# A quarter of the probability-value products moved from VectorE to GpSimd, tiles 2 to 7 of a decoder layer

## The chip, the cores and the metric

The kernel runs on one core of a Trainium2 chip. A core has TensorE (PE, matrix products), VectorE (DVE, elementwise work and reductions), ScalarE (ACT, activations and copies), GpSimd (POOL, elementwise work and the issuing of some transfers) and SyncE (SP, here only a queue that issues transfers). Each engine works through its own queue in order; semaphores make one wait for another. On-chip data lie in SBUF, 128 partitions wide, and results of TensorE in PSUM, in eight banks. The metric is the time of one execution on the device in microseconds, and the number quoted is the median of several runs.

## The reference

One decoder layer on x of 2 x 512 tokens with 1024 features, all in fp32: three sublayers, each added to its input and normalised.

- Attention inside each token. Every token has q of 32 dimensions by 32 heads and k, v of 32 dimensions by 8 heads, each head repeated four times. The scores of a token are a 32 x 32 matrix over pairs of dimensions, summed over the heads.
- A product with a context of 1024 x 1024 per batch, both sides quantised to 256 levels.
- A feed-forward layer: relu squared of an up product (2048 wide) into a down product, plus a latent path scaled by the sum of the two largest routing logits, and a layer norm with gamma and beta.

```
q = einsum('bse,edh->bsdh', x, Wq) + bq          # k, v alike, then repeated 4 times over heads
scores = einsum('bsdh,bseh->bsde', q, k) / sqrt(D)
attn = softmax(scores, axis=-1)
out = einsum('bsde,bseh->bsdh', attn, v)         # the product that the change touches
x = layernorm(x + out)
x = layernorm(x + fake_quant(x) @ fake_quant(ctx))
x = layernorm(x + ffn(x))
```

## The kernel before

The 1024 tokens are eight tiles of 128, one token per partition. Since the repeated heads are equal, q is summed over each group of four, so that scores and outputs need only 8 groups (G = 8, D = 32).

*Token path, tile by tile* (`token_path`). `scores` makes four products of q and k, each [128, 2048] (eight dimensions d, 32 dimensions e, eight groups g; L452, tiles named `pqk`), and reduces each over g (L458) into `s`, a [128, 32, 32] tile. `exponentials` takes row maxima (L467), subtracts them (L468) and lets ScalarE exponentiate `s` in place (L471). `attend` sums the exponentials into `den` (L477), takes reciprocals (L479), and makes four products of probabilities and values, again [128, 2048] each (L485, tiles named `pav`): chunk c has the eight dimensions d from 8c, for all g and e. Each is reduced over e (L491) into `o`. L496 divides by `den`; L506 adds `o` to the tile `xc` and sums its rows. All this is VectorE's, apart from the exponentials. The `pqk` and `pav` tiles share two buffers (tag `prod`).

From tile 2 on the normalisation is mostly ScalarE's (`normalise_aside`): `parts` (L324), squares (L329), `ve` (L331), then a power to -1/2 of one element per partition on GpSimd (`rstd`, L333), `shift` (L337) and one pass over the tile (L338). `cross` quantises the tile on ScalarE (L353, L356, L359, L622), lets TensorE turn the codes (`pta`, L630), copies them (L631), multiplies with the context (`py`, L643), and VectorE adds the result to `xc` (L636, L637, L648). A second normalisation follows, and `transpose_f32` lets TensorE turn the tile for the feed-forward layer (L134).

*Feed-forward blocks.* Two tiles make a block. Blocks 0 and 1 go through `ffn`: sixteen "up" products of eight matmuls each (`pu`, L805) into two PSUM banks (`ps_mm`), emptied by ScalarE (relu L821, square L822), four latent products (L834, and L835 on VectorE), then the down products (`pd`, L1035), whose results VectorE normalises (L302, L984, L991). Blocks 2 and 3 go together through `ffn_pair` (L920) and `down_pair` (L1296) in a scheme with fewer multiplications.

*What sets the order.* The program is written as generators. Tiles 0 and 1 run beside the projections and other preparatory products; then the loop at the end of the kernel emits the feed-forward products of blocks 0 and 1 and advances the token path of tiles 2 to 7 by estimated weights, so that both stand interleaved. The Tile framework then schedules each engine's queue by its own estimates of durations; `tc.issue_after` pins some instructions behind others. TensorE's products are pinned to the order in which they are written. GpSimd's queue also issues transfers: `qk` and `v` of the tile two ahead (L175, L176), context tiles (L536), `ln_beta` onto a finished tile (L715) and outputs (L1019).

The pool `more` is opened between the front part and the feed-forward blocks, that is before tile 2's products, and closed after tile 7. Before the change it holds one tile, a third buffer for down weights (tag `wc`).

Of the kernel before, what the change touches and what calls it, by code (L numbers as in the profile page):

```python
# [9 lines left out]
F32 = mybir.dt.float32  # L10
# [6 lines left out]
P = 128  # L17
# [10 lines left out]
def kernel(  # L28
# [24 lines left out]
    nc = tc.nc  # L53

    B, S, E = x.shape
    _, D, H = wq.shape
    G = wk.shape[2]
# [15 lines left out]
    DC = 8  # L73
# [25 lines left out]
    tokp = tokens_only.enter_context(tc.tile_pool(name="tok", bufs=1, side="right"))  # L99
# [127 lines left out]
    for k in range(KE):  # L227

        pool, tag = (work, "work") if k % 3 == 0 else (xpool, "xc")
# [81 lines left out]
    def normalise(t, name):  # L311

        mean, rstd = mean_rstd([t[:, ts(h, HALF)] for h in range(E // HALF)], name)
        return nc.vector.tensor_scalar(t, t, mean, rstd, ALU.subtract, ALU.mult)

    def normalise_aside(t, sums, name):

        n = sums.shape[-1]
        parts = small.tile([P, 2], F32, tag="parts", name=f"parts_{name}")
        minus = parts[:, 0:1]  # L320
        if n > 1:
            minus = small.tile([P, 1], F32, tag="minus", name=f"minus_{name}")
        with behind_acted(True):
            nc.scalar.activation(  # L324
                parts[:, 0:n], sums, AF.Copy, scale=-1.0 / E, accum_out=minus if n > 1 else None
            )
        square = attp.tile([P, E], BF16, tag="square", name=f"square_{name}")
        total = small.tile([P, 1], F32, tag="square", name=f"squares_{name}")
        nc.scalar.activation(square, t, AF.Square, bias=minus, accum_out=total)  # L329
        ve = small.tile([P, 1], F32, tag="ve", name=f"ve_{name}")  # L330
        nc.scalar.activation(ve, total, AF.Identity, scale=1.0 / E, bias=eps)  # L331
        rstd = small.tile([P, 1], F32, tag="rstd", name=f"rstd_{name}")
        nc.gpsimd.tensor_tensor(rstd, ve, neg_half, ALU.pow)  # L333
        yield 3.0
        shift = small.tile([P, 1], F32, tag="shift", name=f"shift_{name}")
        with behind_acted(True):
            nc.scalar.activation(shift, rstd, AF.Identity, scale=minus)  # L337
        return nc.scalar.activation(t, t, AF.Identity, scale=rstd, bias=shift)  # L338
# [136 lines left out]
    def attend(t, xc, s, v):  # L475
        den = small.tile([P, D], F32, tag="den", name=f"den_{t}")
        nc.vector.tensor_reduce(den, s, AX.X, ALU.add)  # L477
        rden = small.tile([P, D], F32, tag="rden", name=f"rden_{t}")
        nc.vector.reciprocal(rden, den)  # L479
        yield 2.0  # L480

        o = tokp.tile([P, D, G], F32, tag="o", name=f"o_{t}")
        for c in range(D // DC):
            prod = tokp.tile([P, DC * D * G], F32, tag="prod", name=f"pav_{t}_{c}", bufs=2)
            nc.vector.tensor_tensor(  # L485
                prod.rearrange("p (d g e) -> p d g e", d=DC, g=G),
                s[:, ts(c, DC), :].unsqueeze(2).to_broadcast([P, DC, G, D]),
                v.unsqueeze(1).to_broadcast([P, DC, G, D]),
                ALU.mult,
            )  # L490
            nc.vector.tensor_reduce(  # L491
                o[:, ts(c, DC), :].rearrange("p d g -> p (d g)"),
                prod.rearrange("p (c e) -> p c e", e=D), AX.X, ALU.add,
            )
            yield 4.6
        nc.vector.tensor_tensor(o, o, rden.unsqueeze(2).to_broadcast([P, D, G]), ALU.mult)  # L496

        x3 = xc.rearrange("p (c j) -> p c j", j=J)
        o3 = o.rearrange("p d g -> p (d g)").unsqueeze(2).to_broadcast([P, DG, J])
        if t == TB - 1:  # L500

            nc.vector.tensor_tensor(x3, x3, o3, ALU.add)
            normalise(xc, f"1_{t}")
        else:
            sums = small.tile([P, 1], F32, tag="sum1", name=f"sum1_{t}")
            nc.vector.scalar_tensor_tensor(x3, x3, 1.0, o3, ALU.mult, ALU.add, accum_out=sums)  # L506
            yield 1.0
            yield from normalise_aside(xc, sums, f"1_{t}")
        yield 3.0
# [151 lines left out]
    def token_path():  # L661
# [25 lines left out]
        for blk in range(NBLK):  # L687
            xcs = []
            x2T = []
            for i in range(TB):  # L690
# [4 lines left out]
                if t == 0:  # L695

                    begin(1)
                    yield next(at[1][2])
                yield from attend(t, xc, done[t], v)
                if t % (S // P) == 0:  # L700
                    b = t // (S // P)
# [677 lines left out]
    pools = {}  # L1379
# [13 lines left out]
    while not ready:  # L1393
        w_tok += advance()
        while rest is not None and w_fill < w_tok:
            more = next(rest, None)
# [69 lines left out]
```

## Time and profile before

| | |
|---|---|
| median of 3 runs | 709.88 us (708.75 to 710.86) |
| span of the profiled execution | 709.9 us |
| `pav` products, L485 | 32 of 2283 ns, 72.5 us |
| their reductions, L491 | 32 of 2266 ns, 72.0 us |
| `pqk` products, L452 | 32 of 2286 ns, 72.5 us |
| small powers on GpSimd, L333 | 21 of 1049 ns on average, 22.0 us |
| "up" products, L805 (`pu`) | 512 records, 113.4 us |
| granted TensorE clock, mean over the span | 0.989 |

The profile is of one execution. Its page gives busy time per engine, then the span in 40 equal slices (each digit is the busy share in tenths), the transfers, the chain of work that ended last and the costliest groups of instructions. A group's row reads: line, engine, operation, output <- inputs, shape, count, busy time and mean duration, and the idle time of the engine in front of it with what ended it. A row of waits reads: who waited on which line for whom, then total us, times, longest. A timeline row reads: start, duration, engine, line, operation, and in brackets the idle time ahead of it and what ended that. A merged row (x2) spans two instructions.

TensorE records each fp32 matmul of the program as two. An engine's busy time on records that overlap is counted once, so that the start-to-start spacing of like instructions is shorter than their duration: two [128, 2048] products on VectorE take 4.49 us, one 2.28.

### The profile page before, as it was taken

What the parts mean: (1) busy time and instruction counts of PE and PEld (TensorE: products, weight loads), DVE (VectorE), ACT (ScalarE), POOL (GpSimd) and SP (SyncE); (2) the same over time, 40 slices, a digit from 0 to 9 for tenths busy, and PEclk for the clock granted to TensorE, in tenths of its full rate; (3) what the DMA queues carried; (4) which work ended last, traced back from release to release, by engine and by line L of the source; (5) the groups of instructions that cost most, each with busy time, mean ns of one, the idle gap of its engine ahead of it and who ended that gap; (6) DMA issues with size and microseconds to landing.
All of it is one profiled execution on the core that took longest, in us unless ns stands there. A gap on an engine that the chain in (4) does not pass through costs nothing. (4 is left out here: it accounts for less than half of the span.)

```text
span 709.9 us, 7428 instructions
## 1 busy us (share of the span) xinstructions
PE 682.9 (96%) x2794; PEld 482.8 (68%) x2794; DVE 587.8 (83%) x678; ACT 262.5 (37%) x440; POOL 78.0 (11%) x107
## 2 busy tenths in 40 slices
PE   6999999999999999999999999989999999999991
PEld 3666654578876444478876444568888888888881
DVE  5799977699999999799999940587677689897785
ACT  2197644322636459426726041122251200000342
POOL 1011212100011122001001000120010000000012
PEclk9999999999999999999999999999999999999996
DMA  9989719395446558346437435697696444557643
GB/s 333 301 253 367 216 23 295 99 301 161 143 133 171 178 195 257 136 158 228 124 118 195 161 119 165 212 275 261 236 338 229 173 153 150 175 180 198 216 90 119
DMA packets 70901, 139.08 MB, mean 196 GB/s; under 512 B 5265, under 2 KB 39697, under 8 KB 70865
## 3 DMA queue, kind: packets, MB, share of 16 engines
q1 hardware_dynamic: 60656, 106.87, 44.7%
q0 software_dynamic: 10064, 31.47, 16.3%
q8 instruction: 22, 0.36, 0.2%
q10 hardware_dynamic: 144, 0.26, 0.1%
q14 instruction: 15, 0.11, 0.1%
HBM read 114.99 MB, written 21.50 MB: 192 GB/s over the span
## 5 line engine op out<-in xcount | busy, mean ns | idle before, releaser
L1035 PE MATMUL pd<-dn,h 128*128 128x512 f32 x320 | 138.9, 592 | 0.0
L805 PE MATMUL pu<-x2T,up 128*128 128x256 f32 x512 | 113.4, 380 | 0.8 <-ACT relu L821 0.8
L1035 PEld LDWEIGHTS pd<-dn,h 128*128 128x128 f32 x320 | 60.3, 190 | 72.7 <-issue 72.2
L805 PEld LDWEIGHTS pu<-x2T,up 128*128 128x128 f32 x512 | 96.4, 190 | 15.2 <-ACT relu L821 1.2
L452 DVE TENSOR_TENSOR pqk<-qk 128x2048 f32<-128x2048 f32 x32 | 72.5, 2286 | 0.0
L485 DVE TENSOR_TENSOR pav<-s,v 128x2048 f32<-128x2048 f32 x32 | 72.5, 2283 | 0.0
L458 DVE TENSOR_REDUCE s<-pqk 128x256 f32<-128x2048 f32 x32 | 72.4, 2281 | 0.1
L491 DVE TENSOR_REDUCE o<-pav 128x64 f32<-128x2048 f32 x32 | 72.0, 2266 | 0.0
L153 PE MATMUL pqk<-wqkv,xT 128*128 128x512 f32 x128 | 66.1, 619 | 1.8 <-DVE wqkv L233 1.5
L158 PEld LDWEIGHTS pv<-wqkv,xT 128*128 128x128 f32 x128 | 24.3, 190 | 24.2 <-issue 22.5
L333 POOL TENSOR_TENSOR rstd<-ve,neg_half 128x1 f32<-128x1 f32 x21 | 22.0, 1049 | 145.2 <-ACT ve L331 141.9
L158 PE MATMUL pv<-wqkv,xT 128*128 128x256 f32 x128 | 35.6, 379 | 0.0
L153 PEld LDWEIGHTS pqk<-wqkv,xT 128*128 128x128 f32 x128 | 24.7, 198 | 13.9 <-issue 8.0
L821 ACT ACTIVATE relu<-pu 128x256 f32<-128x256 f32 x32 | 12.1, 377 | 52.0 <-PE pu L805 52.0
L643 PE MATMUL py<-cq,aT 128*128 128x512 bf16 x128 | 28.9, 379 | 0.9 <-ACT aT L631 0.9
L1200 DVE TENSOR_TENSOR tt<-dn 128x1024 f32<-128x1024 f32 (+1 forms) x20 | 21.2, 1062 | 9.7 <-DMA dn<-tw 4.4
L436 PE MATMUL pe<-fc,exT 128*128 128x512 f32 x64 | 28.7, 594 | 0.0
L805 PE MATMUL pl<-x2T,fc 128*128 128x256 f32 x128 | 28.2, 380 | 0.3 <-ACT latent L834 0.3
L805 PEld LDWEIGHTS pl<-x2T,fc 128*128 128x128 f32 x128 | 24.2, 190 | 4.0 <-ACT latent L834 0.7
L631 ACT COPY aT<-pta 128x1024 bf16<-128x1024 bf16 x7 | 7.0, 1006 | 50.7 <-PE pta L630 50.7
L643 PEld LDWEIGHTS <-aT 128*128 128x128 bf16 x128 | 12.3, 98 | 16.7 <-ACT aT L631 1.7
L302 DVE BATCH_NORM_STATS2 stats_f<-pd 128x6 f32<-128x512 f32 x8 | 5.3, 686 | 20.4 <-PE pd L1035 20.4
(309 smaller groups left out, 1169.8 us busy)
## 6 DMA issues: line engine op xcount, KB each, us to landing
up<-in_L_ffn_up_w_dram SPq DMA_DIRECT2D x16, 1024.0 KB, 5.8
dn<-in_L_ffn_down_w_dram SPq DMA_DIRECT2D x16, 1024.0 KB, 4.9
pair<-in_L_ffn_up_w_dram SPq DMA_DIRECT2D x8, 1024.0 KB, 5.5
dn<-tw SPq DMA_DIRECT2D x8, 1024.0 KB, 5.1
tw<-outer POOLq DMA_DIRECT2D x7, 1024.0 KB, 4.5
fc<-in_L_ffn_fc_w_dram SPq DMA_DIRECT2D x6, 1024.0 KB, 5.7
dn<-in_L_ffn_down_w_dram SPq DMA_DIRECT2D x12, 512.0 KB, 5.3
outer<-in_L_ffn_down_w_dram SPq DMA_DIRECT2D x5, 1024.0 KB, 5.0
```

Source lines behind the costliest of these rows:

```text
L153: projecting[0] = nc.tensor.matmul(pqk, xT[:, k, :], wqkv[k][:, 0 : 2 * DG], start=(k == 0), stop=(k == KE - 1))
L158: nc.tensor.matmul(pv[:, :DG], xT[:, k, :], wqkv[k][:, 2 * DG : 3 * DG], start=(k == 0), stop=(k == KE - 1),)
L333: nc.gpsimd.tensor_tensor(rstd, ve, neg_half, ALU.pow)
L436: expert[0] = nc.tensor.matmul(ps, exT[m // 2][:, m % 2, ts(l, P)], fc2[m // 2][:, m % 2, ts(n, HALF)], start=(m == 0), stop=(m == NL - 1),)
L452: nc.vector.tensor_tensor(prod.rearrange("p (d e g) -> p d e g", d=DC, g=G), q3[:, ts(c, DC), :].unsqueeze(2).to_broadcast([P, DC, D, G]), ...
L458: nc.vector.tensor_reduce(s[:, ts(c, DC), :].rearrange("p d e -> p (d e)"), prod.rearrange("p (c g) -> p c g", g=G), AX.X, ALU.add,)
L485: nc.vector.tensor_tensor(prod.rearrange("p (d g e) -> p d g e", d=DC, g=G), s[:, ts(c, DC), :].unsqueeze(2).to_broadcast([P, DC, G, D]), ...
L491: nc.vector.tensor_reduce(o[:, ts(c, DC), :].rearrange("p d g -> p (d g)"), prod.rearrange("p (c e) -> p c e", e=D), AX.X, ALU.add,)
L643: crossed[t] = nc.tensor.matmul(py, aT[:, k, :], cq[:, k, ts(h, HALF)], start=(k == 0), stop=(k == KC - 1))
L805: lately[0] = nc.tensor.matmul(ps[:, :NB], ws[:, k, wcols], xT[:, k, :], start=(k == 0), stop=(k == KE - 1))
L1035: lately[0] = nc.tensor.matmul(pd[i][n], h[:, kk // 4, i, kk % 4, :], w[:, k, ts(n, HALF)], start=(kk == 0), stop=(kk == NK - 1),)
L1200: nc.vector.tensor_tensor(tt[:, 0:2], w[:, :, 0::3, :].rearrange("p j q n -> p q j n"), b12.unsqueeze(1).to_broadcast([P, 2, nj, QW]), ALU ...
```

## The change

In `attend`, for every tile for which the pool `more` is open (tiles 2 to 7), the fourth chunk's product is issued on GpSimd, ahead of the other three in the program, into a buffer of its own in `more` (tag `aside`, one buffer of 8 KB per partition). The other three products stay on VectorE with their two shared buffers, and all four reductions stay on VectorE. For tiles 0 and 1 nothing changes. What is computed is the same.

```
         o = tokp.tile([P, D, G], F32, tag="o", name=f"o_{t}")
-        for c in range(D // DC):
-            prod = tokp.tile([P, DC * D * G], F32, tag="prod", name=f"pav_{t}_{c}", bufs=2)
-            nc.vector.tensor_tensor(
+        aside = D // DC - 1 if "more" in pools else None
+        prods = {}
+
+        def product(c):
+            beside = c == aside
+            pool, tag, bufs = (pools["more"], "aside", 1) if beside else (tokp, "prod", 2)
+            prods[c] = prod = pool.tile(
+                [P, DC * D * G], F32, tag=tag, name=f"pav_{t}_{c}", bufs=bufs
+            )
+            (nc.gpsimd if beside else nc.vector).tensor_tensor(
                 prod.rearrange("p (d g e) -> p d g e", d=DC, g=G),
                 s[:, ts(c, DC), :].unsqueeze(2).to_broadcast([P, DC, G, D]),
                 v.unsqueeze(1).to_broadcast([P, DC, G, D]),
                 ALU.mult,
             )
+
+        if aside is not None:
+            product(aside)
+        for c in range(D // DC):
+            if c != aside:
+                product(c)
+            prod = prods.pop(c)
             nc.vector.tensor_reduce(
```

In the changed file the products stand on line 492, their reductions on line 505, and everything behind that is 14 lines lower.

## The prediction

> **What bounds the kernel now.** I read the engine totals and their forty slices first, then what TensorE waits for between 120 and 430 us, then the timelines of VectorE, GpSimd and ScalarE around tile 2.
>
> ```profile
> span 709.9 us, 7428 instructions
> ...
> PE 682.9 (96%) x2794; PEld 482.8 (68%) x2794; DVE 587.8 (83%) x678; ACT 262.5 (37%) x440; POOL 78.0 (11%) x107
> ...
> PE   6999999999999999999999999989999999999991
> ...
> DVE  5799977699999999799999940587677689897785
> ```
>
> TensorE is busy from end to end; VectorE is full only from about 135 to 414 us, where it does the attention of tiles 2 to 7 beside the feed-forward products. In that stretch TensorE waits only 2.3 us:
>
> ```profile
> PE py L643 <- ACT aT L631: 0.9, 1, 0.9
> PE pu L805 <- ACT relu L821: 0.8, 1, 0.8
> PE pl L805 <- ACT latent L834: 0.3, 1, 0.3
> PE pta L608 <- DVE a L344: 0.3, 1, 0.3
> ```
>
> All four come from ScalarE or VectorE, so making VectorE shorter can win about 2 us at most; making it later can cost more, if lateness reaches TensorE through ScalarE, which empties TensorE's two banks of the "up" products (`pu`). GpSimd has only small arithmetic, and the timelines show what it does beside VectorE:
>
> ```profile
> 209.55 2.45 POOL L333 TENSOR_TENSOR rstd<-ve,neg_half 128x1 f32<-128x1 f32 x1 [14.79 <-ACT ve L331]
> ```
> ```profile
> 207.08 4.49 DVE L485 TENSOR_TENSOR pav<-s,v 128x2048 f32<-128x2048 f32 x2
> 211.49 0.42 DVE L835 TENSOR_TENSOR h<-latent,rwb 128x256 f32<-128x256 f32 x1
> ```
>
> The same one-element power takes 0.56 us at 302.23, beside statistics read from PSUM. Here it began in the second of two VectorE products (207.08 to 211.57) and ended at 212.00, 0.43 us after it; those at 230.29, 261.43 and 277.87 end 0.42 to 0.43 us after a product too. So a GpSimd operation is held up by a running VectorE product of two SBUF operands. That the reverse holds, this trace can't show: its GpSimd operations are too short.
>
> **The change.** In the built program tiles 2 to 7 each have one product on GpSimd: six leave VectorE (L485 x32 becomes x26). TensorE's and SP's orders are unchanged. The eight-element-row reduction of each GpSimd product stays on VectorE, and stands last or last but one. The buffer is a new one; nothing else gives up room, and no DMA is added: 0 us.
>
> *Removed.* A product costs 2.20 us start to start (four of them with four reductions fill 17.6 us): 6 x 2.20 = 13.2 us of VectorE.
>
> *The GpSimd product, X us.* No row has it. Floor: VectorE's own 2.28 us. The nearest row by engine is the affine select over 128x128, 0.317 us; less 0.098 us for a 128x1 memset it is 0.219 us per 128 elements, so 2048 take 3.5 us, and with the 0.55 us of a small two-operand operation 4.0 us. Ceiling: the second operand is read on its own, 7.0 + 0.55 = 7.5 us. I take 4.0, from the only row that reads and writes a tile.
>
> *The hold-up.* GpSimd's product and VectorE's `den` both wait for the exponentials:
>
> ```profile
> 157.38 1.22 DVE L477 TENSOR_REDUCE den<-s 128x32 f32<-128x1024 f32 x1 [1.12 <-ACT s L471]
> 158.52 2.28 DVE L485 TENSOR_TENSOR pav<-s,v 128x2048 f32<-128x2048 f32 x1
> ```
>
> GpSimd therefore starts during `den`, 1.14 us before VectorE's first product. If the hold-up works both ways, that product waits X - 1.14; the tile nets X - 1.14 - 2.20 = X - 3.34, +0.66 us at 4.0. Bounds: -2.20 (no hold-up) and +4.16 (X = 7.5). I take both ways: the rows show one engine kept out by the other's operands, and none shows VectorE passing a GpSimd operation under way.
>
> On this the Trainium skill, "SBUF — State Buffer", section "Who interferes with whom", says that a VectorE instruction with two SBUF inputs and a GpSimd one that reads SBUF exclude each other for the whole instruction, whichever began first holding. "GPSIMD Engine Reference", section 3.1, gives 4497 ns for a two-operand operation on 2048 fp32 elements; with that X the sum below would be about 727 us, and both pages speak against this change.
>
> *The new queues.* What matters more than 0.66 us is what now stands ahead of what. ScalarE's queue is reordered in the changed program (it assumes an early end of each tile), and GpSimd's has a product ahead of a small power. An "up" product takes TensorE 3.45 us and needs the bank two products back.
>
> ```profile
> 180.91 0.38 ACT L821 ACTIVATE relu<-pu 128x256 f32<-128x256 f32 x1 [2.62 <-PE pu L805]
> 181.33 0.42 ACT L822 ACTIVATE h<-relu 128x256 f32<-128x256 f32 x1
> 182.91 0.20 ACT L324 ACTIVATE parts<-sum 128x1 f32<-128x1 f32 x1 [1.16 <-DVE xc L506]
> 183.14 1.15 ACT L329 ACTIVATE square<-xc,parts 128x1024 bf16<-128x1024 f32 x1
> ```
>
> 1. Tile 2. `parts` and `square` now stand ahead of that relu (fifth pair, second half). `parts` moves to 183.57, the relu ends at 185.43 instead of 181.29; TensorE wants its bank at 180.91 + 3.45 = 184.36: 1.1 us idle. The next relu now stands behind `shift` (rstd), L338 and L353. GpSimd's power, ready at 185.75, falls into VectorE's second `pqk` product (185.65 to 187.94) and ends near 188.37; two passes of 1.27 and `shift` put the relu's end at 191.5; TensorE is ready at 185.4 + 3.45 = 188.9: 2.6 idle (0.6 without that wait). One more relu behind L356, L359 and L622: 0.5. The wait of 0.86 at 201.03 goes, since TensorE is later. Net +3.4.
> 2. Tiles 3 and 4. Before, `xc_3` was normalised by 266.41 and TensorE transposed it at 266.49: no slack. Now ScalarE's `parts` of tile 4 (waits for L506) stands ahead of tile 3's `shift`. Tile 4's `den` starts 2 x 0.66 late, at 246.0; its products wait until 250.0; three products, four reductions, L479, two L648, L496, a `pqk` product and L506 end at 270.9. From L356 to the end of L338 took 3.5 us before (262.91 to 266.41): done at 274.6. TensorE comes at 266.49 + 3.4 = 269.9: +4.7, in all 8.1.
> 3. Second block's start. ScalarE, held there to 270.9, ends its exponentials of tile 5 at 295.8 instead of 290.37 (its 26.4 us from 262.91 to 289.33 less 1.25 for L622, now behind, and 1.6 idle). L648 of tile 4 has the wait of 2.86, a reduction and a `pqk` product (2.20 each) ahead of it and one product less: 5.4 + 5.1 = 10.5 late, to 327.9. Behind it stands ScalarE's chain to two relus: ends at 330.1 and 336.0 (to 337.8 if a power meets a product). TensorE wants them at 321.1 + 8.1 = 329.2 and 333.55: 0.9 + 2.5 to 4.2, less the old 0.78. I take +3.5, in all 11.6.
> 4. Tile 6. Tile 5's power now stands on GpSimd behind tile 6's product, and tile 5's `shift` ahead of a relu on ScalarE. The exponentials stand behind a relu of 339.94 + 11.6, so end at 353.6; product 4.0, then the power behind VectorE's first product 2.6, then 4.4 of ScalarE: 364.6. TensorE is ready at 339.94 + 3 x 3.45 + 11.6 = 361.9: +2.7, in all 14.3.
>
> Tile 7 costs nothing: its codes are ready at 429 and turned at 453.37, 24 us of cover, gone only if VectorE alone fell that far back. GpSimd's DMA issues that stand behind a product (`v`, `qk` for two tiles later) move by at most 4 us and have some 20 us of cover; without it they would delay `pqk`. From 466 us on all is TensorE's as before. The profiled execution's span is 709.9 us, nothing lies around it, and the median of the runs is 709.88. Sum: 709.9 + 3.4 + 4.7 + 3.5 + 2.7 = 724.2, **724 us**. Each us of X moves it by about 5: step 1 by one, 2 by two (three `den` or products less TensorE's own lateness), 3 and 4 by one each.
>
> **Rivals.**
> - *VectorE isn't held up; GpSimd alone gives way.* For it: only that direction is in the rows. VectorE gains 2.20 per tile, but TensorE gets only its waits back (0.86 + 0.78 + 0.28 = 1.9), and step 4 remains: without lateness the power behind a 4.0 us product ends the relu at 351.0 against 350.3, 0.7. 708.7 us.
> - *Faster: the same with a quick product, X = 2.3.* Step 4 goes too: 708.0, and some of the 2.25 us wait of the last transposes would have to go as well to be below 707.8. It decides only if X is below 3.3 and VectorE runs undisturbed; TensorE's 96% speaks against more.
> - *Held up, but X = 2.3.* 724.2 - 1.7 x 5 = 715.7.
> - *Held up and X = 7.5.* 724.2 + 3.5 x 5 = 741.7.
> - *The change doesn't do what it says:* excluded, the six products stand in GpSimd's queue.
>
> **How the numbers follow.** Held up both ways 0.79, of which X from 2.3 to 3.3: 0.12, 3.3 to 5.6: 0.60, above: 0.07. One-sided with X near 4 or more 0.15; with a quick X 0.06. Range: leaving out those above 735 us (X over 6.1, 0.06) and below 709 (about 0.12) gives 709 to 735; the likeliest case's own range is 716 to 732. About 0.3% (2.1 us) can be told from no change. Slower: 0.79 and a little of the one-sided case, 0.80; same 0.14; faster 0.06.
>
> **What would show it.** Right: L492 products on VectorE with a first one per tile of about X + 1.1 us or a gap of 2.9 after `den`; GpSimd rows of 128x2048 near 4 us; TensorE waits for ScalarE's relu near 184, 189, 330 to 340 and 365 us and for `xc` near 270. Step 1 fails if the relu comes before 184.4; step 2 if L506 of tile 4 ends before 266; step 4 if the power is not behind the product. Wrong altogether: first products of 2.28 us right behind `den`, with TensorE's waits unchanged.

## The result, and the profile after

The changed kernel takes 727.23 us (median of 4 runs, 725.11 to 728.20) against 709.62 (four runs) for the kernel before on the same chip: 1.0238 times as long, 95% interval 1.0222 to 1.0254. Forecast were 724.0 us and "slower" with a chance of 0.80. The profiled execution has a span of 725.3 us and a time of 727.1.

The lines of the page that answer to those shown before (span, busy time per engine, slices, and three groups: VectorE's products of probabilities and values, GpSimd's, and the reductions; in a group the columns are shape and count, busy time and mean duration, idle time ahead):

```profile
span 725.3 us, 7422 instructions
...
PE 685.1 (94%) x2794; PEld 484.8 (67%) x2794; DVE 595.2 (82%) x672; ACT 262.2 (36%) x440; POOL 104.4 (14%) x113
...
PE   6999999999999988998899999989999999999991
...
DVE  5799896899999999699799960197777688897894
...
L492 DVE TENSOR_TENSOR pav<-s,v 128x2048 f32<-128x2048 f32 x26 | 79.8, 3083 | 0.0
...
L505 DVE TENSOR_REDUCE o<-pav 128x64 f32<-128x2048 f32 x32 | 71.7, 2264 | 0.0
...
L492 POOL TENSOR_TENSOR pav<-s,v 128x2048 f32<-128x2048 f32 x6 | 27.5, 4591 | 35.6 <-ACT s L471 35.6
```

Six products left VectorE, and yet it is busy for 595.2 us instead of 587.8: its other 26 products take 3083 ns on average instead of 2283. The reductions are what they were. GpSimd's product takes 4.6 us.

The timelines of VectorE and GpSimd at tile 2 show where those 800 ns come from:

```profile
156.68 1.22 DVE L477 TENSOR_REDUCE den<-s 128x32 f32<-128x1024 f32 x1 [1.12 <-ACT s L471]
157.82 5.57 DVE L492 TENSOR_TENSOR pav<-s,v 128x2048 f32<-128x2048 f32 x1
```
```profile
156.73 4.51 POOL L492 TENSOR_TENSOR pav<-s,v 128x2048 f32<-128x2048 f32 x1 [7.24 <-ACT s L471]
```

GpSimd's product ends at 161.24; VectorE's first one, begun at 157.82, ends 2.15 us after that, about its own length (2.28 alone). It was kept out for the rest of the other. The second and third products of the tile take 2.28.

What TensorE waits for between 120 and 430 us (total, times, longest); it was 2.3 us before:

```profile
PE pu L819 <- ACT relu L835: 6.8, 5, 3.1
PE pt_x L134 <- ACT xc L338: 6.6, 1, 6.6
PE pl L819 <- ACT latent L848: 0.3, 1, 0.3
PE pu L819 <- DMA up<-in_L_ffn_up_w_dram: 0.3, 1, 0.3
PE pta L622 <- DVE a L344: 0.2, 1, 0.2
```

Both large ones are ScalarE's. TensorE's timeline has them at these places:

```profile
185.10 3.72 PE L819 MATMUL pu<-x2T,up 128*128 128x256 f32 x16 [1.08 <-ACT relu L835]
...
274.94 1.97 PE L134 MATMUL pt_x<-ident,xc 128*128 128x128 f32 x8 [6.56 <-ACT xc L338]
...
338.05 22.68 PE L819 MATMUL pu<-x2T,up 128*128 128x256 f32 x96 [2.14 <-ACT relu L835]
363.82 7.17 PE L819 MATMUL pu<-x2T,up 128*128 128x256 f32 x32 [3.10 <-ACT relu L835]
```

The second line holds something that the forecast had no term for: eight transposes take 1.97 us here and 1.07 before. The windows of the changed kernel (stretch, its length, busy times of PE, PEld, DVE, ACT and POOL, granted clock, DMA share, GB/s) show TensorE at half its clock behind that wait and behind the one at 338:

```profile
274.94:280.24 5.30, 5.30 (x13) 3.23 (x14) 5.30 (x4) 5.30 (x7) 0.89 (x1) 0.50 0.53 131
280.24:283.60 3.36, 3.36 (x9) 1.50 (x8) 3.36 (x2) 3.36 (x5) 0.55 (x1) 0.99 0.77 163
338.34:341.75 3.41, 3.41 (x9) 2.66 (x9) 3.41 (x3) 2.21 (x8) 1.35 (x1) 0.50 1.07 345
341.75:345.20 3.45, 3.45 (x17) 3.04 (x16) 3.45 (x2) 2.31 (x4) 0.58 (x1) 1.00 0.26 103
363.82:367.20 3.38, 3.38 (x16) 2.99 (x17) 2.92 (x3) 3.11 (x6) 0.00 (x0) 1.00 0.47 162
```

At 0.50 the eight transposes take nearly twice as long, so about half of such a stretch is lost: 2.65 us of the first and 1.71 of the third.

### The profile page after: what moved, and what is told of

It is laid out like the page before. It is cut to its first block, busy times and chain, and to the rows that moved or that the text cites. A ratio compares the mean times of both kernels' runs of the same rounds, so it can differ in the third digit from the quotient of the medians.

```text
span 725.3 us, 7422 instructions
## 1 busy us (share of the span) xinstructions
PE 685.1 (94%) x2794; PEld 484.8 (67%) x2794; DVE 595.2 (82%) x672; ACT 262.2 (36%) x440; POOL 104.4 (14%) x113
## 5 line engine op out<-in xcount | busy, mean ns | idle before, releaser
L1049 PE MATMUL pd<-dn,h 128*128 128x512 f32 x320 | 140.7, 599 | 0.0
L819 PE MATMUL pu<-x2T,up 128*128 128x256 f32 x512 | 115.9, 385 | 7.1 <-ACT relu L835 6.8
L492 DVE TENSOR_TENSOR pav<-s,v 128x2048 f32<-128x2048 f32 x26 | 79.8, 3083 | 0.0
L492 POOL TENSOR_TENSOR pav<-s,v 128x2048 f32<-128x2048 f32 x6 | 27.5, 4591 | 35.6 <-ACT s L471 35.6
```

The costliest lines, as they stand in the source:

```text
L492: (nc.gpsimd if beside else nc.vector).tensor_tensor(prod.rearrange("p (d g e) -> p d g e", d=DC, g=G), s[:, ts(c, DC), :].unsqueeze(2).to ...
L819: lately[0] = nc.tensor.matmul(ps[:, :NB], ws[:, k, wcols], xT[:, k, :], start=(k == 0), stop=(k == KE - 1))
L1049: lately[0] = nc.tensor.matmul(pd[i][n], h[:, kk // 4, i, kk % 4, :], w[:, k, ts(n, HALF)], start=(kk == 0), stop=(kk == NK - 1),)
```

## The experiments

Theory: the two engines' products exclude each other, so each tile ends about 1 us late, and ScalarE's and GpSimd's queues, whose new order counts on tiles that end early, pass that on to TensorE several times over. (VectorE's own queue is reordered with them; where the text speaks of the order, it means all three.) Rivals: the new order of the queues is the whole loss; the lateness is the whole loss, whatever the order; any long GpSimd operation slows VectorE; each tile costs a sixth.

### GpSimd only writes

```
-            (nc.gpsimd if beside else nc.vector).tensor_tensor(
+            if beside:
+                nc.gpsimd.tensor_copy(prod[:, 0:1], s[:, 0, 0:1])
+                nc.gpsimd.memset(prod, 0.0)
+                nc.gpsimd.memset(prod, 0.0)
+                return
+            nc.vector.tensor_tensor(
```

> The changed kernel, with GpSimd's product replaced by work of its own that writes the same tile without reading operands of that size: a copy of one element per partition from the probabilities, which makes GpSimd wait for the exponentials as the product does, and two fills of the 128x2048 tile. The last quarter of the products is left out (zeros). The order of the other engines' queues is that of the changed kernel. Theory (the products of VectorE and GpSimd keep each other out because both read from SBUF): a tile that is only written holds nobody up, VectorE's first products take 2.28 us again instead of 5.5, the six tiles end about 2.2 us earlier than before instead of 1.2 later, and TensorE loses nothing in steps 1 to 3: 707 to 711 us. Rival (the new order of ScalarE's and GpSimd's queues is what costs, whatever VectorE does): still 720 or more. Rival (any long GpSimd operation slows VectorE): first products above 4 us, 720 or more.

Measured: 711.54 us against 710.35 before on that chip, ratio 1.0025 (1.0001 to 1.0049). GpSimd writes from 156.42 to 160.08, beside VectorE's first product, which is not touched (its timeline):

```profile
156.14 1.22 DVE L477 TENSOR_REDUCE den<-s 128x32 f32<-128x1024 f32 x1 [1.12 <-ACT s L471]
157.28 2.28 DVE L497 TENSOR_TENSOR pav<-s,v 128x2048 f32<-128x2048 f32 x1
```

So a long GpSimd operation that only writes costs VectorE nothing, and the new order, with every tile 2.2 us early, costs 1 to 2 us, not 17. The upper end of the expectation, 711, was passed by half a us, and TensorE does lose in step 3. Its waits between 120 and 430 us in this kernel:

```profile
PE pu L824 <- ACT relu L840: 3.5, 1, 3.5
PE pta L627 <- DVE a L344: 0.2, 1, 0.2
```

This relu, at the second block's start, ends 0.97 us later than before (326.50 instead of 325.53), although every tile's VectorE work is 2.2 us shorter; TensorE arrives earlier and so waits longer. A kernel that leaves out six products altogether, with the queues in the new order, isn't faster than the kernel before: with this order there was nothing to be won from VectorE. With the old order that was not run.

### The extra product, with the old order

```
         o = tokp.tile([P, D, G], F32, tag="o", name=f"o_{t}")
+        if "more" in pools:
+            idle = pools["more"].tile([P, DC * D * G], F32, tag="aside", name=f"aside_{t}", bufs=1)
+            nc.gpsimd.tensor_tensor(
+                idle.rearrange("p (d g e) -> p d g e", d=DC, g=G),
+                s[:, ts(3, DC), :].unsqueeze(2).to_broadcast([P, DC, G, D]),
+                v.unsqueeze(1).to_broadcast([P, DC, G, D]),
+                ALU.mult,
+            )
```

> The kernel before, with all four products of a tile on VectorE, and from the third tile on the fourth one made a second time by GpSimd, at the place where the change has it, into a tile that nobody reads. The queues of the other engines keep the order of the kernel before. Theory (hold-up): VectorE's first product of each of the six tiles takes 5.5 us instead of 2.28 with nothing taken off VectorE, so each tile is some 3.3 us later than before against 1.2 in the changed kernel; at four to five us of loss for each us of tile 728 to 742 us, though the order of the queues is the old one. Rival (the new order of the queues costs): at most 712.

Measured: 725.53 us, ratio 1.0207 (1.0175 to 1.0239); below the 728 expected, far above 712. First products take 5.47 to 5.59 us in tiles 2 to 6 with nothing taken away, so those tiles are 3.2 to 3.3 us late. The waits of TensorE between 120 and 430 us are other ones than the changed kernel's:

```profile
PE pt_x L134 <- ACT xc L338: 5.7, 1, 5.7
PE pl L813 <- ACT latent L842: 3.8, 1, 3.8
PE pu L813 <- ACT relu L829: 1.7, 2, 1.4
PE py L651 <- ACT aT L639: 1.7, 1, 1.7
```

Lateness alone can cost this much, but it took three times the lateness of the changed kernel. The next run makes the lateness equal.

### Half an extra product, with the old order

The same edit on a tile of 128x1024: `DC // 2` dimensions, `s[:, ts(7, DC // 2), :]`.

> The kernel before, with all four products on VectorE and, from the third tile on, half a product (128x1024) made in addition by GpSimd into a tile that nobody reads, at the place where the change has its product. The queues of the other engines keep the order of the kernel before. GpSimd's half should take 2.2 to 2.5 us, so that VectorE's first product of a tile is held up by some 1.2 us: each tile is late by about as much as in the changed kernel (5.5 us for the first product less the product taken away), but with the old order of the queues. Theory (the lateness of the tiles and the new order of ScalarE's and GpSimd's queues work together; the order decides how much of it reaches TensorE): 713 to 719 us. Rival (the lateness alone makes the loss, the order has no part in it): 724 to 728. Rival (1.2 us a tile is covered as long as the order is the old one): 709 to 711.

Measured: 713.38 us against 709.93, ratio 1.0040 (1.0017 to 1.0063). GpSimd's half takes 2.39 us on average; the first product of a tile is held to 3.31 to 3.42, 1.0 to 1.1 us more than alone; at tile 2 (GpSimd, then VectorE):

```profile
155.73 2.36 POOL L485 TENSOR_TENSOR aside<-s,v 128x1024 f32<-128x1024 f32 x1 [7.24 <-ACT s L471]
156.81 3.42 DVE L493 TENSOR_TENSOR pav<-s,v 128x2048 f32<-128x2048 f32 x1
```

In the changed kernel a tile is late by 5.46 to 5.58 less 2.28 less the 2.20 saved, also 1.0 to 1.1. The four runs side by side:

| VectorE's tiles 2 to 6 | old order of the queues | order of the changed kernel |
|---|---|---|
| 2.2 us early | not run | +0.25% (only writes) |
| as before | 0 | not run |
| 1.0 to 1.1 us late | +0.40% (half extra) | +2.38% (the change) |
| 3.2 to 3.3 us late | +2.07% (extra) | not run |

Neither rival stands as the whole loss: the new order with early tiles gives 0.25%, this lateness with the old order 0.40%, both together 2.38%. What the order costs with tiles neither early nor late was not run, so the table doesn't split the loss into two parts. It allows another reading: if each order is laid out for the products that its own program leaves on VectorE, the changed kernel's tiles are 3.2 to 3.3 us behind that plan, as late as the extra product makes them behind the old one, and the two lose alike, some 2.1% over their own kernel with undisturbed products. By that reading the new order counts on 2.2 us that the hold-up takes away. It fits the runs, and none tests it by itself. The GpSimd operation is also half as long here, so that a power that would wait behind it is part of what this run leaves out.

### The product beside the sums

```
-        if aside is not None:
-            product(aside)
         for c in range(D // DC):
-            if c != aside:
+            if aside is None:
                 product(c)
+            elif c == 0:
+                product(0)
+                product(1)
+                room = pools["more"].tile([P, DC * D * G], F32, tag="aside", name=f"aside_{t}", bufs=1)
+                with tc.issue_after(made_by[1].ins):
+                    nc.vector.memset(room[:, 0:1], 0.0)
+                product(aside, room)
+            elif c == 2:
+                with tc.issue_after(summed_o[0].ins):
+                    product(2)
```

> The changed kernel, with the tile's work put in another order: VectorE makes two products, then writes one element per partition of GpSimd's tile, on which GpSimd waits, then sums the two products while GpSimd makes its own; the third product comes behind the two sums. Theory: a sum reads one operand, and isn't kept out; GpSimd's product of 4.55 us fits beside two sums (4.4 us) but for 0.2 us, all VectorE products take about 2.3 to 2.5 us, each tile ends some 2 us earlier than before, TensorE gets its small waits back and the power behind GpSimd's product costs up to 1: 707 to 711 us. Rival (GpSimd's reads keep out every VectorE operation on SBUF): the sums take 4 us or more, 720 or more. Rival (order of the queues): 718 or more.

Measured: 715.04 us, ratio 1.0064 (1.0046 to 1.0083): 12 us better than the change, with the same work on both engines and the changed kernel's order on ScalarE, but outside the 711 expected and still slower than the kernel before. All products on VectorE are back at 2278 ns, and the sums run beside GpSimd's product at 2.28. What was not foreseen is in VectorE's timeline at tiles 2 and 5, where other small operations stand in between:

```profile
162.64 2.28 DVE L514 TENSOR_REDUCE o<-pav 128x64 f32<-128x2048 f32 x1
...
164.83 2.65 DVE L798 COPY rwm<-rw 128x128 f32<-128x128 f32 x1
...
294.52 2.28 DVE L514 TENSOR_REDUCE o<-pav 128x64 f32<-128x2048 f32 x1
296.72 3.63 DVE L661 SCALAR_TENSOR_TENSOR xc<-xc,r,crow 128x1024 f32<-128x1024 f32 x1
```

GpSimd's products lie at 162.89 to 167.41 and 294.76 to 299.27. The copy of 0.22 us ends just after GpSimd does, the two-operand addition of 1.28 some 1.1 us after: both were kept out until GpSimd's product was done. TensorE's largest wait is again that for the relu at the second block's start, 3.9 us, as where GpSimd only wrote.

### GpSimd copies: one operand

```
-            (nc.gpsimd if beside else nc.vector).tensor_tensor(
+            if beside:
+                nc.gpsimd.tensor_copy(
+                    prod.rearrange("p (d g e) -> p d g e", d=DC, g=G),
+                    s[:, ts(c, DC), :].unsqueeze(2).to_broadcast([P, DC, G, D]),
+                )
+                return
+            nc.vector.tensor_tensor(
```

> The changed kernel, with GpSimd's product replaced by a copy of the probabilities spread over the same 128x2048 tile: one operand read instead of two. The last quarter of the products is therefore wrong by the missing factor v. The queues of all engines keep the order of the changed kernel. It asks what of GpSimd's product keeps VectorE out. Theory (that it reads SBUF at all): VectorE's first product of a tile still ends some 2.2 us behind the end of GpSimd's copy; with a copy of 2 to 3 us it takes 3 to 4.2 us, each tile is from 1.2 us early to level with the kernel before, and the time is 711 to 718 us. Rival (only a second operand collides): first products of 2.28 us, 709 to 713, as where GpSimd only wrote.

Measured: 713.37 us in one run. At tile 2 (GpSimd, then VectorE):

```profile
156.58 1.89 POOL L493 COPY pav<-s 128x2048 f32<-128x2048 f32 x1 [7.21 <-ACT s L471]
157.69 2.93 DVE L498 TENSOR_TENSOR pav<-s,v 128x2048 f32<-128x2048 f32 x1
```

GpSimd's copy ends at 158.47, and VectorE's first product, 157.69 to 160.62, ends 2.15 us after it, as behind the product. One operand read from SBUF is enough; the rival is out.

### Tile 7 alone, tile 2 alone, all but tiles 3 and 4

In each the condition of `aside` is narrowed: `t == NT - 1`, `t == 2`, `t not in (3, 4)`.

> The change for tile 7 alone; tiles 2 to 6 are as before. Theory (what a late tile costs depends on what TensorE waits for there, and tile 7 has 24 us of cover): its first product takes 5 to 7 us, and the time is within 0.3% of the kernel before, 709.0 to 711.0. Rival (each tile costs about a sixth of the 17 us, wherever it stands): 712.5 to 713.0.

Measured: 710.66 us, ratio 0.9996 (0.9976 to 1.0016). The expected price of nothing held, the place of the hold-up did not: GpSimd's product began at 389.47 and caught another two-operand sum, ahead of `den` (timeline of VectorE):

```profile
389.78 4.89 DVE L889 TENSOR_TENSOR ss<-ss,pair 128x512 f32<-128x512 f32 x1
394.59 1.21 DVE L477 TENSOR_REDUCE den<-s 128x32 f32<-128x1024 f32 x1
395.72 0.14 DVE L650 TENSOR_TENSOR r<-total,s12d 128x1 f32<-128x1 f32 x1
395.79 2.28 DVE L492 TENSOR_TENSOR pav<-s,v 128x2048 f32<-128x2048 f32 x1
```

VectorE lost 4.2 us there (such a sum takes 0.68 alone), and the time shows none of it, which agrees with the 24 us of cover.

> The change for tile 2 alone: step 1 of the prediction by itself. Theory: TensorE waits for ScalarE's relu near 184 to 193 us, 1.5 to 2.7 us in all less the wait of 0.86 for the codes' copy that it had before, and keeps that lateness except for the 0.78 at the second block's start: 711 to 713 us, against 713.3 by the prediction's 3.4 us for this step. Rival (the lateness of tile 2 is made up later): 709.9.

Measured: 711.33 us, ratio 1.0023 (1.0009 to 1.0037), 1.4 to 1.6 us. TensorE waits 1.41, 0.28 and 0.20 us for the relu at 185 to 193 us, and no longer 0.86 for the codes' copy; 0.7 more is lost at `xc` near 268. It is the prediction's step 1 by itself, at half the size that it had there.

> The change for tiles 2, 5, 6 and 7, tiles 3 and 4 as before: step 2 of the prediction is taken out. Theory: TensorE's wait of 6.6 us for the normalised tile 3 near 275 us goes, and with it the lower clock behind it (some 2.5 us); steps 1 and 4 stay, step 3 shrinks as VectorE comes to it on time: 712 to 719 us. Rival (the loss is spread over the tiles evenly, a third less without these two): 721 to 722.

Measured: 721.01 us, ratio 1.0166 (1.0143 to 1.0190). The theory's 712 to 719 is missed and the rival's figure is met, but the loss isn't even. TensorE's timeline, in the order of steps 1, 2, 3 and 4 and one wait further on:

```profile
185.38 3.72 PE L819 MATMUL pu<-x2T,up 128*128 128x256 f32 x16 [1.39 <-ACT relu L835]
...
268.87 1.09 PE L134 MATMUL pt_x<-ident,xc 128*128 128x128 f32 x8 [0.71 <-ACT xc L338]
324.83 3.72 PE L819 MATMUL pu<-x2T,up 128*128 128x256 f32 x16 [1.08 <-ACT relu L835]
331.90 22.67 PE L819 MATMUL pu<-x2T,up 128*128 128x256 f32 x96 [3.35 <-ACT relu L835]
354.89 7.17 PE L819 MATMUL pu<-x2T,up 128*128 128x256 f32 x32 [0.31 <-ACT relu L835]
390.42 1.15 PE L134 MATMUL pt_x<-ident,xc 128*128 128x128 f32 x8 [1.72 <-ACT x2T L135]
```

The wait of 6.56 is down to 0.71, as meant. Step 3 grows from 2.14 to 4.4 in its place, with 1.7 us at the low clock behind it. Its relu still comes 6 us later than before, with tiles 3 and 4 on time: tile 5's `den` begins at 289.63 (290.41 before), but its first product takes 5.58, and the queue has more of tile 5 ahead of tile 4's additions, which end at 322.5 instead of 317.4. So step 3 needs no lateness from tiles 3 and 4; a stall taken away ahead of it uncovers it. Stalls at one engine are not a sum of independent prices.

### What an idle of TensorE costs besides itself

```
+                held_back = IDLES.get((blk, c, i), 0)
+                if held_back:
+                    junk = pools["more"].tile([P, E], F32, tag="aside", name=f"junk_{blk}_{c}", bufs=1)
+                    for _ in range(held_back):
+                        with tc.issue_after(acted[0].ins):
+                            acted[0] = nc.scalar.activation(
+                                junk, ps[:, 0:1].to_broadcast([P, E]), AF.Identity
+                            )
```

> The kernel before, with six stops of TensorE put in: ahead of the relu of six up products ScalarE runs 5, 6, 8 (first block) and 4, 7, 9 (second block) extra passes of 1.1 us over a scratch tile, so that the bank comes free late and TensorE idles by about 1 to 7 us. It asks what an idle of TensorE costs besides itself. Theory, from the rows behind the idles of the runs so far (clock 0.50 behind 6.6, 5.7, 3.8 and 2.1 us, but 1.00 behind 3.1, 3.5 and 3.9): idles above about 4 us are followed by some 4 to 6 us at a clock near half, shorter ones sometimes; the loss behind one is 1.5 to 2.8 us. Rival (a stop costs only its own length): the clock behind all six stays 1.00.

Measured: 747.88 us in one run. TensorE's idles at the six stops were 1.54, 3.21, 6.13, 1.20, 4.27 and 6.55 us; the four longer ones are followed by a clock of 0.50, the other two not. The rival is out. Two windows of this kernel, behind the stop of 3.21:

```profile
184.88:188.30 3.42, 3.42 (x10) 2.70 (x9) 3.42 (x3) 1.30 (x3) 1.94 (x1) 0.50 0.00 0
188.30:191.71 3.41, 3.41 (x17) 3.02 (x16) 3.41 (x3) 2.85 (x5) 0.49 (x1) 1.00 0.39 84
```

My threshold of 4 us was wrong; what decides stands in the last section.

## Why the prediction was right, and where it wasn't

The sum was 14.3 us; the spans of the two profiled executions differ by 15.4, the medians by 17.6. By its steps, in us of TensorE's lateness read from when the same instruction starts in the two traces:

| step | forecast | measured |
|---|---|---|
| front part and first products | 0 | -0.7 |
| 1, relu of tile 2 | +3.4 | +2.4 |
| 2, transposes of `xc_3` | +4.7 | +6.7 |
| low clock behind it | none | +2.6 |
| 3, second block's start | +3.5 | +1.4 |
| low clock behind it | none | +1.7 |
| 4, power behind tile 6's product | +2.7 | +3.1 |
| to the end | 0 | -1.8 |
| sum | 14.3 | 15.4 |

*The hold-up* works both ways, as taken: shown by the first products of 5.5 us and by the runs in which GpSimd wrote or copied. The row from which it was argued (the held-up power) pointed the right way. Only the row that it was set against was misread: the power at 302.23 ran beside L984's pass over `pd` (302.06 to 303.46), not beside statistics. The rule of the Trainium skill ("SBUF — State Buffer", "Who interferes with whom") agrees on each point that a run here touches: two-operand operations of VectorE are kept out by a GpSimd operation that reads, not by one that writes, and reductions are free. The page also lists copies as able to collide, which the copy of 2.65 us instead of 0.22 bears out.

*X* was mis-sized: 4.0 from the affine select, 4.5 to 4.6 measured (4.84 in tile 7). By the prediction's own slope of 5 that is 2.5 to 3 us of the final sum. The figure that the Trainium skill ("GPSIMD Engine Reference", section 3.1) gives (4497 ns) was closer than the row.

*Step 1.* The relu did stand behind `parts` and `square`, and came at 185.04 (forecast 185.43). The second wait, 2.6 us with a bound of 0.6, was 0.27: the power (185.31, 0.58 us) wasn't held by a VectorE product. The third was 0.20 instead of 0.5. In the 2.4 are two waits that the step didn't have, 0.25 for a weight load and 0.26 for a latent product's copy, and about 0.27 for each restart (a product of 3.72 us instead of 3.45).

*Step 2.* `xc` was ready at 274.9 (forecast 274.6). The wait was longer because TensorE came 1.5 us earlier than forecast, step 1 being smaller and the front quicker.

*Step 3.* The exponentials of tile 5 came as forecast (VectorE's `den` follows them at 295.58; forecast 295.8, though the terms given for it add to 295.5). The two relus ended at 330.4 and 338.0 (forecast 330.1 and 336.0, or 337.8 where a power meets a product, which it did: 332.66, 2.29 us). TensorE's idle was 2.1 rather than 0.9 + 2.5 to 4.2, since it arrived later by step 2 and the low clock.

*Step 4.* GpSimd's timeline has the power as forecast, right behind the product and held up:

```profile
352.36 4.51 POOL L492 TENSOR_TENSOR pav<-s,v 128x2048 f32<-128x2048 f32 x1 [8.18 <-ACT s L471]
356.83 2.61 POOL L333 TENSOR_TENSOR rstd<-ve,neg_half 128x1 f32<-128x1 f32 x1
```

The relu ended at 363.8 (forecast 364.6).

*What failed* is a missing term: what a stall does to the clock behind it, 4.3 us in all. "From 466 us on all is TensorE's as before" missed the same thing in the other direction: before, the wait of 2.25 us near 465 was followed by half clock, and in the changed kernel (482) it wasn't: 1.4 of the -1.8 us. The old wait of 0.28 for the latent copy, gone with its restart, is 0.5; what follows behind cancels (1.4 us less in TensorE near 681, 1.4 more in the passes behind TensorE's last product).

"The profiled execution's span is 709.9 us, nothing lies around it" was wrong too: every execution of both kernels whose span and time are listed has a time 1.8 us above its span (727.12 and 725.3, 709.94 and 708.2). The profiled execution of before was thus, by estimate, some 711.7 us, 1.8 above the median then known, and since the sum was laid on 709.9, which is also the median, the slip did not show in the 724; it is why the medians differ by 2 us more than the spans.

So the times at which ScalarE would be done came out within 0.8 us in steps 2 and 4 and within 0.3 us of the bounds in step 3. How long TensorE would wait for them did not, because each wait is the difference of two times, and TensorE's own lateness was counted without the clock. That the total was met within 0.5% owes something to errors of opposite sign.

## What to carry to other kernels

Before moving a large elementwise operation to GpSimd, look at what VectorE does during it: beside two-operand work both stand still in turn, and beside reductions GpSimd's product holds nothing up (715.0 against 727.2 us here for the same split, though 0.6% more than without the change). Ask whether the bottleneck waits for the engine that is relieved at all; here leaving the six products out, in the order of queues that came with the change, was worth nothing. And when a scheduler lays out queues by estimated durations, an operation that ends later than it believes can cost more than its own lateness: 1 us a tile cost about 3 us in the old order and 17 in the new one, whose plan, as far as the runs tell, counted on each tile ending 2.2 us earlier.

## What the runs showed of the hardware that was not expected

TensorE's low clock comes in fixed portions at fixed times. In the kernel with the six stops the clock falls at 184.88, 201.95, 283.87, 365.79, 389.68 and 502.32 us: each pair is a multiple of 3.413 us apart, to within 0.03. It stays at 0.50 for one such portion (3.41 us, 1.71 lost if TensorE is busy) or two. Laying that grid through the eleven traces and adding up TensorE's idle time inside each portion (from 40 to 685 us), 2.07 us or more in one portion was always followed by a drop at its end, and 1.97 or less at full clock never. Two portions followed where the first one at half clock held 1.46 us of idle or more, and one where it held 0.23 or less. So the length of an idle doesn't decide alone: 2.14 us at 336 in the changed kernel lay in one portion and cost 1.71 more; 3.10 us at 361 were cut into 1.51 and 1.59 and cost nothing, and neither did the 3.89 before the relu in the kernel with the product beside the sums, cut into 1.97 and 1.91.

The Trainium skill ("TensorE: Matmul & The Clock Gate", "What's actually happening") has the portion: a free-running window of 3413 ns, a length that the traces confirm to the last digit they show. Its advice to keep gaps below about 3 us ("Why this matters for your kernels") is too generous here, as 2.14 us was enough. Whether an idle meets one portion or two should change from one execution to the next; that the scatter of the runs (710.7 to 716.0 us for the kernel with half an extra product, clock 0.993 to 0.987) comes from there was not tested.
